# Row sums of the adjacency one graph earlier, and an earlier transpose of x1, in a two-layer graph network

## Chip, cores and metric

The kernel runs on one core of a Trainium2 chip. The metric is the device time of one execution in microseconds (us); the median of three runs is compared. The core has five engines with queues of their own: TensorE (PE, matmuls and transposes), VectorE (DVE), ScalarE (ACT), GpSimd (POOL) and SyncE (SP, which here only issues transfers).

## What is computed

64 graphs, each with 256 nodes of 256 features. Cut to what matters (`bn` is a batch norm with fixed statistics):

```python
# layer 0
deg = adj.sum(-1); deg = where(deg != 0, deg, 1.0)
d = deg ** -0.5
a_plus = d[:, :, None] * adj * d[:, None, :] + alpha * eye
x1 = layernorm(x + (a_plus @ x) @ W.T + b)
# layer 1
h = relu(bn1(conv1d(x1, 1 tap)));  h = bn2(conv1d(h, 17 taps))
x_conv = relu(h + x1)                       # along the nodes
s = x1 @ w_se.T + b_se                      # 3 columns
A = exp(-(|s_i|^2 + |s_j|^2 - 2 s_i.s_j))   # 256 x 256
x_nmp = A @ relu(x1 @ w_msg.T + b_msg)
x2 = GRU(input=concat(x_conv, x_nmp), state=x1)
out = layernorm(x1 + x2)
```

## The kernel before

**Stages.** The 64 graphs make four quarters of 16 (Q = 16). Each quarter goes through three kinds of work. First its *graphs*: layer 0 and the parts of layer 1 up to the spectrum of h. Then the *products*: the 17-tap convolution is done for all 16 graphs at once in a transformed domain, with `p_k` (L545) as its matmuls. Then the *gates*: the GRU, with `p_g` (L872) as its matmuls and a layernorm at its end. The stages of neighbouring quarters are interleaved: some graphs of the next quarter run beside products and their transforms (VectorE operations on the tile VM, L600 to L755), some beside gates of the quarter in front. In graphs 0 to 15 the place of gates is taken by the transform of the weights (`p_u`, L308). After graph 63 only the last quarter's products and gates are left.

**One graph.** `layer0(g)` is a generator in pieces that end with `yield`:

- Piece 1. The row sums (L358): two ScalarE activations that copy a half of adj to an unused place and add up each row into `deg`. The guard (L369, DVE): where the sum is 0 it becomes 1. The power `dis` (L371, POOL), deg to the power of -0.5. `adeg` (L373, DVE), alpha times deg. Four transposes `p_adjT` (L380, PE), their copy (L381, ACT), two DVE operations that put the diagonal in (L383, they need adeg), the scaling of x into `x1` (L393, ACT, twice, it needs dis), and x plus its bias (L394, POOL).
- Piece 2. `p_hT` (L401, eight matmuls, which need x1 and adjT with its diagonal), its copy (L406, ACT).
- Piece 3. `p_out0` (L411, eight matmuls, which need hT), and its two evictions into x1 (L416, DVE, which scale by dis).
- Pieces 4 and 5. The layernorm: statistics (L326 to L328, DVE), a power (L329, POOL), then L332 (DVE) and two activations (L334, ACT), and the store of x1 (L422).

`layer1(g)` has seven pieces: the transpose of x1 (`x1_transposed`, L425: four transposes `p_x1T`, L431; copies L432 and L433, ACT) | `p_conv` (L448) with the evictions L451 and L452 (ACT) and the squares of s (L456, L458, L459, DVE) | `p_msg` (L469, relu L472) | `p_dft` (L486, copies L491) | `p_rows` (L499, copies L501 and L503) | `p_dist` (L510, exp L511 on ACT, product with adjT L512 on DVE) | `p_nmp` (L519, copy L523, store L524 issued from ACT's queue).

**What sets the order.** Nothing is sorted by cost. The order of each engine's queue is that in which the generators are stepped, except where `tc.issue_after(i)` puts an instruction behind instruction i of the same engine's queue (an order, not a wait). `graphs()` (L994) steps layer1(g) and, between its pieces, steps layer0(g + 2) at places listed in PLACES (L990):

```python
PLACES = (("other",), ("layer0",), (), (), ("layer0",), ("other", "layer0"), ())
```

So row sums and transposes of adj for graph g + 2 come behind conv, p_hT behind p_rows, p_out0 behind the gates ("other") that follow the distances, the layernorm's statistics at the end of the graph (STATS) and its end in the following graph behind the relu L472 (APPLIED). PE's order in a graph is, for most graphs: p_rows, p_hT, p_dist, gates, p_out, p_nmp, p_x1T, gates, half of p_conv, p_adjT, the other half, p_msg, p_dft. In graphs 16 to 27 (the set ALONE, which stand beside no gates) p_x1T of the next graph comes between p_out and p_nmp. The row sums of graph g + 2 are put behind EVICTED[g], the last L452 of graph g, but are free to come earlier in ALONE graphs and in graphs below 16.

**Buffers.** The matmul tiles of a graph (`p_adjT`, `p_hT`, `p_out0`, `p_x1T`, `p_conv`, `p_msg`, `p_dft`, `p_rows`, `p_dist`, `p_nmp`) share four PSUM buffers in turn: a tile waits until the fourth in front of it has been read. adj_t and x_t have two buffers; their loads for graph g + 3 are issued from SP's queue at the start of graph g (L104 to L110). x1, xn, msg and the like have one or two buffers, adjT three.

Of the kernel before, what the change touches and what calls it, by code (L numbers as in the profile page):

```python
# [26 lines left out]
def kernel(  # L27
# [27 lines left out]
    nc = tc.nc  # L55
    B, N, D = x.shape
# [4 lines left out]
    DCH = D // P  # L61
# [6 lines left out]
    Q = P // GT  # L68
# [13 lines left out]
    def bank(name):  # L82
        return ps.tile([P, 512], F32, tag="bank", name=name)
# [7 lines left out]
    def mark(op, gates=0):  # L91
        marks.append((op.ins, gates))
# [226 lines left out]
    def layernorm(y, eps=LN_EPS):  # L319

        chunks = range(y.shape[1])
        st = small.tile([P, NCH, nc.vector.BN_STATS_DIM], F32, name="ln_st")
        mv = small.tile([P, NCH, nc.vector.BN_AGGR_DIM], F32, name="ln_mv")
        rs = small.tile([P, NCH], F32, name="ln_rs")
        for c in chunks:
            nc.vector.bn_stats(st[:, c, :], y[:, c, :])  # L326
            nc.vector.bn_aggr(mv[:, c, :], st[:, c, :])
        nc.vector.tensor_scalar(rs[:, : len(chunks)], mv[:, : len(chunks), 1], eps, None, op0=ALU.add)  # L328
        nc.gpsimd.tensor_tensor(rs[:, : len(chunks)], rs[:, : len(chunks)], neg_half[:, : len(chunks)], op=ALU.pow)  # L329
        yield  # L330
        mr = small.tile([P, NCH], F32, name="ln_mr")
        nc.vector.scalar_tensor_tensor(mr[:, : len(chunks)], mv[:, : len(chunks), 0], -1.0, rs[:, : len(chunks)], op0=ALU.mult, op1=ALU.mult)  # L332
        for c in chunks:
            nc.scalar.activation(  # L334
                y[:, c, :], y[:, c, :], AF.Identity, bias=mr[:, c : c + 1], scale=rs[:, c : c + 1]
            )
# [4 lines left out]
    xn_d = [dram.tile([P, 2 * DCH, N], F32, name=f"xn_d{g}") for g in range(B)]  # L341
    XN = {}
    ALONE = set()
    EVICTED, RELU = {}, {}
    ADJT, X1, X_SCALED, DIAGONAL = {}, {}, {}, {}


    def layer0(g):

        a_t, x_t = ain.pop(g), xin.pop(g)  # L350

        adjT = work.tile([P, NCH, 3, P], F32, name="adjT", bufs=3)
        ADJT[g] = adjT

        deg = small.tile([P, NCH], F32, name="deg")
        def degrees():
            for c in range(NCH):
                nc.scalar.activation(  # L358
                    unused if g >= Q else adjT[:, c, 0:2, :].rearrange("p n q -> p (n q)"), a_t[:, c, :], AF.Copy,
                    accum_out=deg[:, c : c + 1],  # L360
                )

        if g == 1 or g >= Q and g - 2 not in ALONE:

            with tc.issue_after(X_SCALED[0] if g == 1 else EVICTED[g - 2]):
                degrees()
        else:
            degrees()
        nc.vector.scalar_tensor_tensor(deg, deg, 0.0, deg, op0=ALU.is_equal, op1=ALU.add)  # L369
        dis = small.tile([P, NCH], F32, name="dis")  # L370
        nc.gpsimd.tensor_tensor(dis, deg, neg_half[:, :NCH], op=ALU.pow)  # L371
        adeg = small.tile([P, NCH], F32, name="adeg")
        nc.vector.tensor_scalar(adeg, deg, alpha_t, None, op0=ALU.mult)  # L373

        p = bank("p_adjT").rearrange("p (c n) -> p c n", c=NCH)
        for mc in range(NCH):
            for c in range(NCH):
                nc.tensor.transpose(p[:, mc, c * P : (c + 1) * P], a_t[:, c, mc * P : (mc + 1) * P], ident)  # L380
        copied = nc.scalar.copy(adjT[:, :, 0:3:2, :], p.rearrange("p c (n q) -> p c n q", q=P))  # L381
        for mc in range(NCH):
            DIAGONAL[g] = nc.vector.scalar_tensor_tensor(  # L383
                adjT[:, mc, 1, :], ident, adeg[:, mc : mc + 1], adjT[:, mc, 2 * mc, :],
                op0=ALU.mult, op1=ALU.add,
            ).ins


        x1 = work.tile([P, NCH, D], F32, name="x1")
        X1[g] = x1  # L390
        with tc.issue_after(copied.ins) if g < 2 else ExitStack():
            for c in range(NCH):
                X_SCALED[g] = nc.scalar.activation(x1[:, c, :], x_t[:, c, :], AF.Copy, scale=dis[:, c : c + 1]).ins  # L393
        nc.gpsimd.tensor_tensor(x_t, x_t, b0_t.unsqueeze(1).to_broadcast([P, NCH, D]), op=ALU.add)  # L394

        yield
        hT = work.tile([P, DCH, N], F32, name="hT", bufs=1)
        p = bank("p_hT").rearrange("p (k n) -> p k n", k=DCH)
        for k in range(DCH):
            for mc in range(NCH):  # L400
                nc.tensor.matmul(  # L401
                    p[:, k, :], x1[:, mc, k * P : (k + 1) * P],
                    adjT[:, mc, 1 - mc : 3 - mc, :].rearrange("p n q -> p (n q)"),
                    start=mc == 0, stop=mc == NCH - 1,
                )
        nc.scalar.copy(hT, p)  # L406
        yield
        p = bank("p_out0").rearrange("p (c o) -> p c o", c=NCH)
        for c in range(NCH):
            for k in range(DCH):  # L410
                nc.tensor.matmul(  # L411
                    p[:, c, :], hT[:, k, c * P : (c + 1) * P], w0[:, k, :], start=k == 0, stop=k == DCH - 1
                )
        for c in range(NCH):
            mark(
                nc.vector.scalar_tensor_tensor(  # L416
                    x1[:, c, :], p[:, c, :], dis[:, c : c + 1], x_t[:, c, :], op0=ALU.mult, op1=ALU.add
                )
            )
        yield  # L420
        yield from layernorm(x1)
        nc.scalar.dma_start(x1_d[g // Q][g % Q].rearrange("(c p) d -> p c d", p=P), x1)  # L422
        yield

    def x1_transposed(g):  # L425
        x1 = X1.pop(g)
        xn = XN[g] = work.tile([P, 2 * DCH, N], F32, name="xn")
        p = bank("p_x1T").rearrange("p (k n) -> p k n", k=DCH)
        for k in range(DCH):
            for c in range(NCH):  # L430
                nc.tensor.transpose(p[:, k, c * P : (c + 1) * P], x1[:, c, k * P : (k + 1) * P], ident)  # L431
        nc.scalar.activation(xn[:, 0], p[:, 0], AF.Identity, bias=unit, scale=others_only)  # L432
        nc.scalar.copy(xn[:, 2 * DCH - 1], p[:, 1])  # L433

    def layer1(g, place):
# [3 lines left out]
        xn, adjT = XN.pop(g), ADJT.pop(g)  # L439
# [5 lines left out]
        for c in range(NCH):  # L445
            p = bank("p_conv1")[:, : D + NSE]
# [19 lines left out]
        p = bank("p_msg").rearrange("p (c d) -> p c d", c=NCH)  # L466
# [14 lines left out]
        for k in range(DCH):  # L481
            p = bank("p_dft")

            for c, t0, t1 in ((0, 0, mid + 1), (1, mid - 1, GT)):
                first = t0 + 1 - c * mid
# [11 lines left out]
        p = bank("p_rows")  # L497
# [9 lines left out]
        for c in range(NCH):  # L507
            rows = slice(32 * c, 32 * c + 32)
            p = bank("p_dist")[:, :N]
            nc.tensor.matmul(p, dl[rows, c * P : (c + 1) * P], dr[rows, :], start=True, stop=True)  # L510
            nc.scalar.activation(aT[:, c].rearrange("p n q -> p (n q)"), p, AF.Exp, bias=nsq[:, c : c + 1], scale=2.0)  # L511
        mark(nc.vector.tensor_mul(aT, aT, adjT[:, :, 0:3:2, :]))  # L512
        yield
        if g in ALONE:
            x1_transposed(g + 1)
        p = bank("p_nmp").rearrange("p (k n) -> p k n", k=DCH)
        for k in range(DCH):
            for mc in range(NCH):
# [1 line left out]
                    p[:, k, :], msg[:, mc, k * P : (k + 1) * P], aT[:, mc].rearrange("p n q -> p (n q)"),  # L520
                    start=mc == 0, stop=mc == NCH - 1,
                )
        nc.scalar.copy(xn[:, 1 : 1 + DCH], p)  # L523
        nc.scalar.dma_start(xn_d[g], xn)  # L524
        yield

# [427 lines left out]
    def chain(*stages):  # L954
        for stage in stages:
            yield from stage
# [13 lines left out]
    def run(stage):  # L970
        for _ in stage:
            pass
# [18 lines left out]
    STATS, APPLIED = len(PLACES) - 1, 4  # L991
    ENDS = [iter(())]

    def graphs(first, part, others):  # L994


        for i in part:
            load(first + i + 3)
            given = {"layer0": layer0(first + i + 2) if first + i + 2 < B else iter(()), "other": others[i]}
            for piece, _ in enumerate(layer1(first + i, i)):  # L1000
                if piece == APPLIED:
                    with tc.issue_after(RELU[first + i]):
                        run(ENDS.pop())
                    ENDS.append(given["layer0"])
                elif piece == STATS:
                    next(given["layer0"], "end")
                yield
                for name in PLACES[piece]:
                    if next(given[name], "end") != "end":
                        yield  # L1010
            yield from given["other"]

    with tc.tile_pool(name="setup", bufs=1) as setup:
# [52 lines left out]
        others = [weights(setup, i, scale2) for i in range(NPARTS)]  # L1066
# [26 lines left out]
    def nothing():  # L1093
        return iter(())
# [16 lines left out]
    for q in range(NQ):  # L1111
        first = (q + 1) * Q
        more = q + 1 < NQ
        end = chain(complex_end(q), copies(V2) if more else iter(()))
        if more:
            if q:
                others = [take(late, 3 if i % 3 == 0 else 2) for i in range(AHEAD)]
            else:
                others = [nothing() for _ in range(AHEAD)]
# [24 lines left out]
        if more:  # L1144
# [6 lines left out]
            others = [take(early, 5 if q == 0 else 2) for _ in range(Q)]  # L1151
# [63 lines left out]
```

## Time and profile before

| what | value |
|---|---|
| median of three runs | 2073.0 us (2072.61 to 2079.12) |
| profiled execution, its own time | 2079.83 us |
| its span in the profile | 2078.0 us |
| mean TensorE clock | 0.991 of full |
| TensorE busy | 1996.5 us |
| graphs 0 to 15 | about 40 to 296 us of the span |
| graphs 16 to 27 | about 296 to 505 us |
| graphs 28 to 31 | about 505 to 610 us, then products and gates to 799 us |
| graphs 32 to 47 | about 799 to 1110 us |
| graphs 48 to 63 | about 1301 to 1611 us |
| the last products and gates | to 2078 us |

How to read it. "Busy" is the time in which an engine executes; its share is an average over stages with different limits. A line of the waits names an engine, its instruction and its source line, then, after the arrow, the engine, tile and line whose end released it, with the total in us, the number of times and the longest. "L393" is line 393 of the kernel before. A group's line gives the instructions of one line and shape, their busy time and mean duration in ns, then the idle time of the engine before them and what ended it. The chain of waits follows the work back from the end: each entry is what the next one waited for.

### The profile page before, as it was taken

How to read it: one execution, taken by the hardware profiler on the slowest of the kernel's cores; microseconds unless marked ns; L12 is line 12 of the kernel's file. 1: busy time of each engine (PE TensorE's matmuls, PEld its weight loads, DVE VectorE, ACT ScalarE, POOL GpSimd, SP SyncE). 2: the span in 40 equal slices, each digit the busy share in tenths (PEclk: the TensorE clock that was granted, in tenths of full speed). 3: DMA queues.
4: the chain of work that ended last, by engine and by line, in shares of the span. 5: the costliest groups of instructions: out<-in, count | busy, mean ns of one | idle time of the engine just before them, and what ended most of it. 6: DMA issues, size and time to landing. Idle time of an engine off the chain costs nothing.

```text
span 2078.0 us, 26334 instructions
## 1 busy us (share of the span) xinstructions
PE 1996.5 (96%) x8157; PEld 1444.4 (70%) x8157; DVE 1395.1 (67%) x3241; ACT 937.4 (45%) x2232; POOL 663.7 (32%) x672
## 2 busy tenths in 40 slices
PE   6999999998999999989999999999999999999997
PEld 5888888877677766767777766666777765555554
DVE  5444458776568897753546889774445899977776
ACT  4676644566432234555553223545554123333333
POOL 3444410122432243232322234322332124434443
PEclk9999999999999999999999999999999999999999
DMA  4765657544447644343326664433333754443331
GB/s 122 232 221 184 195 183 226 174 142 146 107 145 216 201 124 125 114 119 109 102 96 184 202 177 123 126 119 104 107 107 114 232 151 128 126 111 99 99 91 52
DMA packets 305288, 298.04 MB, mean 143 GB/s; under 512 B 84192, under 2 KB 283956, under 8 KB 305150
## 3 DMA queue, kind: packets, MB, share of 16 engines
q1 hardware_dynamic: 245198, 200.37, 33.2%
q10 hardware_dynamic: 44480, 67.39, 9.1%
q0 software_dynamic: 15472, 28.61, 6.1%
q8 instruction: 66, 1.08, 0.2%
q14 instruction: 72, 0.59, 0.1%
HBM read 193.19 MB, written 103.06 MB: 143 GB/s over the span
## 4 chain that ended last, share of the span: by engine, by line
PE 48%; DVE 12%; issue 4%; DMA 4%; POOL 3%; ACT 3%; SPq 0%; ACTq 0%; POOLq 0%; DVEq 0%
PE p_g L872 30%; PE p_k L545 7%; PE p_hT L401 3%; PE p_out L411 2%; PE p_nmp L519 2%; DMA u<-ud 2%; POOL sums L843 1%; DVE ln_st L326 1%; PE p_dist L510 1%; PE p_conv L448 1%; DVE VM L733 1%; ACT x L393 1%; POOL dis L371 1%; POOL ln_rs L329 1%; DVE G L927 1%
## 5 line engine op out<-in xcount | busy, mean ns | idle before, releaser
L872 PE MATMUL p_g<-wall,sums 128*128 128x384 f32 x1536 | 536.2, 489 | 5.6 <-DVE G L900 5.5
L872 PEld LDWEIGHTS p_g<-wall,sums 128*128 128x128 f32 x1536 | 284.4, 190 | 193.0 <-issue 12.7
L872 PE MATMUL p_g<-wall,inputs 128*128 128x384 f32 x1152 | 408.1, 490 | 7.2 <-DVE G L890 7.2
L872 PEld LDWEIGHTS p_g<-wall,inputs 128*128 128x128 f32 x1152 | 217.9, 191 | 158.0 <-DVE G L890 14.1
L843 POOL TENSOR_TENSOR sums<-inputs 128x384 f32<-128x384 f32 x128 | 142.7, 1115 | 317.7 <-PE p_g L872 265.6
L329 POOL TENSOR_TENSOR ln_rs<-ln_rs,neg_half 128x2 f32<-128x2 f32 x129 | 95.0, 738 | 400.9 <-DVE ln_rs L328 329.0
L512 DVE TENSOR_TENSOR aT<-aT,adjT 128x512 f32<-128x512 f32 x64 | 47.3, 740 | 229.1 <-ACT aT L511 229.1
L915 ACT ACTIVATE G<-G 128x512 f32<-128x512 f32 x128 | 80.7, 630 | 265.4 <-DVE G L902 154.5
L545 PE MATMUL p_k<-u,VM 128*128 128x256 f32 x736 | 175.3, 381 | 5.0 <-DMA u<-ud 4.9
L545 PEld LDWEIGHTS p_k<-u,VM 128*128 128x128 f32 x736 | 138.7, 190 | 32.4 <-DMA u<-ud 4.2
L401 PE MATMUL p_hT<-adjT,x 128*128 128x256 f32 x512 | 130.8, 400 | 18.0 <-ACT x L393 7.7
L394 POOL TENSOR_TENSOR x_t<-x_t,b_t 128x512 f32<-128x512 f32 x64 | 89.5, 1399 | 158.5 <-issue 92.1
L448 PE MATMUL p_conv<-wc,xn 128*128 128x259 f32 x512 | 125.3, 383 | 6.4 <-ACT xn L432 5.7
L371 POOL TENSOR_TENSOR dis<-deg,neg_half 128x2 f32<-128x2 f32 x64 | 47.5, 743 | 254.1 <-DVE deg L369 251.3
L411 PE MATMUL p_out<-w,hT 128*128 128x256 f32 x512 | 124.6, 387 | 4.1 <-ACT hT L406 3.7
L401 PEld LDWEIGHTS p_hT<-adjT,x 128*128 128x128 f32 x512 | 95.2, 197 | 40.2 <-ACT x L393 10.7
L519 PE MATMUL p_nmp<-aT,msg 128*128 128x256 f32 x512 | 121.6, 380 | 0.2 <-DVE aT L512 0.2
L469 PE MATMUL p_msg<-wmsg,xn 128*128 128x256 f32 x512 | 121.2, 379 | 0.0
L411 PEld LDWEIGHTS p_out<-w,hT 128*128 128x128 f32 x512 | 97.1, 193 | 32.2 <-ACT hT L406 12.8
L486 PE MATMUL p_dft<-fwd,h 128*128 128x240 f32 x512 | 114.4, 366 | 1.9 <-ACT scols L452 1.9
L448 PEld LDWEIGHTS p_conv<-wc,xn 128*128 128x128 f32 x512 | 95.6, 190 | 29.0 <-ACT xn L432 7.5
L843 POOL TENSOR_TENSOR sums<-inputs,sums 128x384 f32<-128x384 f32 x64 | 68.9, 1077 | 133.9 <-PE p_g L872 133.8
(163 smaller groups left out, 3535.7 us busy)
## 6 DMA issues: line engine op xcount, KB each, us to landing
u<-ud SPq DMA_DIRECT2D x284, 256.0 KB
xn_d<-xn ACTq DMA_DIRECT2D x64, 512.0 KB
inputs<-xn_d SPq DMA_DIRECT2D x64, 512.0 KB
ud<-u_set POOLq DMA_DIRECT2D x39, 480.0 KB, 6.2
adj_t<-in_adj_dram SPq DMA_DIRECT2D x64, 256.0 KB
x_t<-in_x_dram SPq DMA_DIRECT2D x64, 256.0 KB
x_d<-x ACTq DMA_DIRECT2D x64, 256.0 KB
xc_d<-VM SPq DMA_DIRECT2D x64, 256.0 KB
```

Of the source, the lines that this page charges most:

```text
L329: nc.gpsimd.tensor_tensor(rs[:, : len(chunks)], rs[:, : len(chunks)], neg_half[:, : len(chunks)], op=ALU.pow)
L394: nc.gpsimd.tensor_tensor(x_t, x_t, b0_t.unsqueeze(1).to_broadcast([P, NCH, D]), op=ALU.add)
L401: nc.tensor.matmul(p[:, k, :], x1[:, mc, k * P : (k + 1) * P], adjT[:, mc, 1 - mc : 3 - mc, :].rearrange("p n q -> p (n q)"), start=mc == ...
L411: nc.tensor.matmul(p[:, c, :], hT[:, k, c * P : (c + 1) * P], w0[:, k, :], start=k == 0, stop=k == DCH - 1)
L448: nc.tensor.matmul(p, x1T[:, k, c * P : (c + 1) * P], wc1[:, k, :], start=k == 0, stop=k == DCH - 1)
L469: nc.tensor.matmul(p[:, c, :], x1T[:, k, c * P : (c + 1) * P], wmsg[:, k, :], start=k == 0, stop=k == DCH - 1)
L486: nc.tensor.matmul(p[:, t0 * FL : t1 * FL], h[:, c, k * P : (k + 1) * P], fwd[:, first : first + t1 - t0, :].rearrange("p t f -> p (t f)") ...
L519: nc.tensor.matmul(p[:, k, :], msg[:, mc, k * P : (k + 1) * P], aT[:, mc].rearrange("p n q -> p (n q)"), start=mc == 0, stop=mc == NCH - 1,)
L545: nc.tensor.matmul(p[:, j * D : (j + 1) * D], v[:, k, :], u[:, k, :], start=k == 0, stop=k == DCH - 1)
L843: nc.gpsimd.tensor_tensor(S[i], x, y, op=op)
L872: nc.tensor.matmul(p[:, : 3 * HD] if k == 0 else p[:, HD:], a[:, k], wall[:, b, k].rearrange("p t d -> p (t d)"), start=first and k == 0, ...
L915: nc.scalar.activation(rz, rz, AF.Tanh, scale=0.5)
```

## The change

Three things change their places; no instruction is added or taken out.

1. The row sums, guard, power and adeg become a piece of layer0 of their own for every graph after the first two. They are issued for graph g + 3 at the end of graph g, after the layernorm statistics of graph g + 2, with the row sums behind AGGREGATED[g], the nmp copy of graph g in ACT's queue. Graph 2's are issued ahead of graph 0. What is left of the first piece (p_adjT, its copy, the diagonal, the scaling of x) stays at its place, two graphs ahead and behind conv, as before.
2. The scaling of x (L393) of graph g is put behind EVICTED[g - 2] in ACT's queue, the last copy of the conv evictions.
3. p_x1T of graph g + 1 with its copies comes behind the distances of graph g, ahead of p_out0, in the graphs of a list (EAGER): 0, 12 to 14, 16 to 28, 37, 38, 53 and 54. In the others it stays at the start of the next graph. ALONE is filled but no longer read.

```diff
-    EVICTED, RELU = {}, {}
+    EAGER = {0, Q - 4, Q - 3, Q - 2, *range(Q, Q + 13), 2 * Q + 5, 2 * Q + 6, 3 * Q + 5, 3 * Q + 6}
+    EVICTED, RELU, AGGREGATED, LAYER0 = {}, {}, {}, {}
...
-        if g == 1 or g >= Q and g - 2 not in ALONE:
-
-            with tc.issue_after(X_SCALED[0] if g == 1 else EVICTED[g - 2]):
-                degrees()
-        else:
+        at = X_SCALED[0] if g == 1 else AGGREGATED.get(g - 3)
+        with tc.issue_after(at) if at else ExitStack():
             degrees()
         nc.vector.scalar_tensor_tensor(deg, deg, 0.0, deg, op0=ALU.is_equal, op1=ALU.add)
         dis = small.tile([P, NCH], F32, name="dis")
         nc.gpsimd.tensor_tensor(dis, deg, neg_half[:, :NCH], op=ALU.pow)
         adeg = small.tile([P, NCH], F32, name="adeg")
         nc.vector.tensor_scalar(adeg, deg, alpha_t, None, op0=ALU.mult)
+        if g > 1:
+            yield
...
-        with tc.issue_after(copied.ins) if g < 2 else ExitStack():
+        with tc.issue_after(copied.ins if g < 2 else EVICTED[g - 2]):
             for c in range(NCH):
                 X_SCALED[g] = nc.scalar.activation(x1[:, c, :], x_t[:, c, :], AF.Copy, scale=dis[:, c : c + 1]).ins
...
         mark(nc.vector.tensor_mul(aT, aT, adjT[:, :, 0:3:2, :]))
-        yield
-        if g in ALONE:
+        if g in EAGER:
             x1_transposed(g + 1)
+        yield
...
-        nc.scalar.copy(xn[:, 1 : 1 + DCH], p)
+        AGGREGATED[g] = nc.scalar.copy(xn[:, 1 : 1 + DCH], p).ins
...
+    def of_layer0(g):
+        if g not in LAYER0:
+            LAYER0[g] = layer0(g) if g < B else iter(())
+        return LAYER0[g]
+
     def graphs(first, part, others):
         for i in part:
             load(first + i + 3)
-            given = {"layer0": layer0(first + i + 2) if first + i + 2 < B else iter(()), "other": others[i]}
+            if first + i == 0:
+                next(of_layer0(2))
+            given = {"layer0": of_layer0(first + i + 2), "other": others[i]}
...
                 elif piece == STATS:
                     next(given["layer0"], "end")
+                    next(of_layer0(first + i + 3), "end")
```

## Prediction on record

> **What bounds the kernel now.** I read the page's busy shares first, then TensorE's waits, then the groups behind the largest waits, then the chain of waits around the worst place.
>
> ```profile
> span 2078.0 us, 26334 instructions
> PE 1996.5 (96%) x8157; PEld 1444.4 (70%) x8157; DVE 1395.1 (67%) x3241; ACT 937.4 (45%) x2232; POOL 663.7 (32%) x672
> ```
>
> TensorE (PE) is busy for 1996.5 of 2078.0 us, so the change, which takes no matmul away, can only work on the 81.5 us in which PE stands, and on stretches in which PE runs slowly. The waits of PE name what ended each idle stretch (sum, times, longest):
>
> ```profile
> PE p_hT L401 <- ACT x L393: 7.7, 9, 1.8
> PE p_g L872 <- DVE G L890: 7.2, 7, 1.6
> ...
> PE p_conv L448 <- ACT xn L432: 5.7, 7, 1.1
> ...
> PE p_hT L401 <- ACT msg L472: 4.7, 18, 0.8
> PE p_rows L499 <- DVE deg L369: 3.9, 2, 2.0
> PE p_hT L401 <- DVE adjT L383: 3.8, 6, 1.3
> PE p_out L411 <- ACT hT L406: 3.7, 6, 0.9
> ```
>
> The first, fourth and fifth belong to the row-sum chain, the third and last to x1's transpose. The gate waits (L890) are mostly in the last stage, where no graph runs; the change does not reach them. The groups behind the first (busy, mean ns | idle of that engine before it, and its releasers):
>
> ```profile
> L393 ACT ACTIVATE x<-x_t,dis 128x256 f32<-128x256 f32 x128 | 60.1, 507 | 47.3 <-POOL dis L371 47.3
> L371 POOL TENSOR_TENSOR dis<-deg,neg_half 128x2 f32<-128x2 f32 x64 | 47.5, 743 | 254.1 <-DVE deg L369 251.3
> ```
>
> ACT stands 47.3 us ahead of the scaling L393 waiting for the power, and POOL stands ahead of the power for the guard L369: the power comes just in time or too late. The chain of waits at the worst place (start, us, what):
>
> ```profile
> 917.64 0.58 ACT xn L432
> 918.27 1.14 PE p_conv L448 x4
> ...
> 922.46 1.37 POOL ln_rs L329 x2
> 923.83 0.97 POOL sums L843
> 924.87 0.99 POOL sums L843
> 926.02 0.72 POOL dis L371
> 926.76 0.52 ACT x L393
> 927.33 3.78 PE p_hT L401 x8
> 931.11 1.16 PE p_dist L510 x4
> ```
>
> In graph 38 PE waits 1.08 us for L432, 1.96 us before p_rows and 0.79 us before p_hT; then the eight p_hT matmuls take 3.78 us, where the same eight take 1.73 us at 961.44. The same picture stands at 1420 to 1429 (graph 54). And as a table of stages (sum; PE, PEld, DVE, ACT, POOL busy; clock):
>
> ```profile
> 296.00:505.00 209.00, 201.73 (x985) 169.00 (x984) 155.94 (x409) 113.18 (x292) 34.30 (x32) 1.00 0.53 171
> 799.00:961.00 162.00, 154.01 (x653) 113.54 (x652) 100.67 (x275) 86.94 (x225) 44.19 (x48) 0.97 0.38 114
> ```
>
> PE stands 7.3 us in graphs 16 to 27 and 8.0 us in graphs 32 to 39. DVE at 156 of 209 us is dense in the first of these stretches.
>
> **What the Trainium skill says.** "Perfetto Trace Analysis", section "Tensor Engine Instruction (MATMUL, LD_WEIGHTS)": ScalarE, VectorE and GpSimd are strict FIFO. The trace agrees: at 923.93 ACT has nothing to do but L393, and L491, whose p_dft was ready by 924.1, starts at 927.58, after it. "TensorE: Matmul & The Clock Gate", "Part 1: The HAM clock gate": after an idle window of about 3.4 us the clock goes to half, and to full again after a busy window; the windows run freely. The trace agrees with that: PE is nearly idle from 924.07 to 927.33 (3.26 us), then runs at half rate from 927.33 to 936.20.
>
> **The change, part by part.** Nothing is added to or taken from any engine's work; the instruction orders of both kernels have equal counts.
>
> *Row sums, guard, power and adeg, one graph earlier.* Each graph's two row sums (430 ns each, with an accumulator read of 0.19 us) now stand behind the nmp copy L523 of the graph three in front. Every instruction counts on its queue:
> - ACT: 2 × (0.43 + 0.19) = 1.24 us between L523 and what followed it, L432/L433 or L451. In a gate graph, 897.39: L523 0.58, L432 0.57, L433 0.37 end at 898.76 and would end at 900.0; conv starts at 901.50. Cover 1.5 us, from 3.9 us of gate matmuls. In graphs 2 to 11 four p_u program matmuls and x1T cover about 3.4 us against a chain of 2.8 us. Price 0; if the cover went, up to 1.2 us a graph.
> - DVE: L369 and L373 (0.15 + 0.25 us) move from beside L383 to behind layernorm's L332, ahead of L456. They could stall the queue until ACT has summed, but ACT is done by nmp's end + 1.9 us, and L332 waits for POOL L329 longer than that anyway (449.01, with nmp's end at 444.75). Price 0 to 0.4 us in graphs 16 to 27.
> - POOL: the power (0.74 us) leaves the place behind sums L843 and comes behind L329.
> - The row sums now need adj(g+3) earlier. Its load is issued 16 us (graph 0), then 24 us or more, before the end of L523 of graph g; the three times ACT waited for it, it came 2.9 to 4.2 us after issue. No wait.
>
> L393 then waits only for its place behind L452. Where its stall goes:
> - p_hT<-x apart from graphs 38 and 54, 7.7 − 2 × 0.79 = 6.1 us: at 887.21 (and 1388) the wait of 1.81 becomes one of 0.9 for L383, next in line on DVE. Gain 6.1 − 1.8 = 4.3.
> - p_hT<-msg, 4.7: L472 stands behind L393 in ACT's queue, as at 979 and 1097. Next late is p_rows, which PE does first. I take 4.0.
> - p_hT<-adjT of graphs 34 and 50, 0.59 and 0.58, and half of p_rows<-ln_mv (0.41 + 0.42): 1.6. The other adjT waits stay.
>
> *x1T between distances and out0.* The four transposes (0.44 us) move ahead of out0 in 21 graphs (in 12 of them, 16 to 27, from between out0 and nmp, in the others from behind nmp).
> - conv<-L432: five waits of 0.70 (49, 240, 253, 268, 515 us) go, since p_out and p_nmp (3.5 us) now stand between transpose and conv: 3.5.
> - out<-hT waits at 263, 401 and 510 (0.78, 0.90, 0.76) are filled by 0.44 of transposes each: 1.3.
> - In graph 0 it also lets part of the 1.7 us wait for taps pass: 0 to 1.7, I take 0.8.
>
> *Graphs 38 and 54, both parts together.* Before: 1.08 + 1.96 + 0.79 = 3.83 us. The conv wait goes, but p_rows then stands ready earlier, and its columns still wait for L458/L459 on DVE, behind L332, behind POOL's L329 and L843. POOL's second inputs move forward there, so I let the columns come 0.7 us earlier (bounds 0 and 1.5) and the 0.79 vanish: 1.5 each, 3.0. The half-rate stretch costs (936.20 − 927.33)/2 ≈ 4.4 us each time; PE would still stand about 2.3 us there around a short p_rows, so I keep it.
>
> *Graphs 16 to 27.* In 16 to 19 products of the transform cover all. In 20 to 27 waits of 1.18, 0.77 and 0.21 for the distances may lose 1.0; the loop out0 → L416 → layernorm → L456 → L383 → p_hT takes 0.44 us more for x1T ahead of out0, against some 0.3 us of L369/L373 out of its middle. Bounds −4 and +4 over the stretch; I take 0.
>
> *New waits.* In graph 27, at 503, row sums join the copies between the two spectrum buffers ahead of L451, and p_dft<-scols (1.92) may grow: +0.5. In graph 37 p_adjT and p_msg wait for banks freed later: +0.35 each place and quarter, +0.7.
>
> Sum: 4.3 + 4.0 + 1.6 + 3.5 + 1.3 + 0.8 + 3.0 − 0.5 − 0.7 = 17.3 us. Made against the profiled execution's own time, 2079.8 (span 2078.0 + 1.8 outside), this is 2062.5; the median of the runs is 2073.0, 6.8 below, and the same waits are in those runs: 2073.0 − 17.3 = 2055.7.
>
> **Rivals.**
> - *The half clock vanishes too* (2046). If PE's idle time near 924 falls apart into less than a window, both half-rate stretches go: 2 × 4.4 = 8.8, so 2055.7 − 8.8 = 2047, with luck in graphs 20 to 27 2046. For it: the idle shrinks from 3.26 us. Against it: the window runs freely and p_rows is only 0.2 us of work; what remains may still fill one.
> - *The waits are moved, not removed* (2067). p_hT then waits for L383, msg or POOL instead of L393, and p_rows for all that conv saved. Only the five conv waits and the fillings of 1.3 and 0.8 remain: 5.6, thus 2067. For it: at 926 the p_rows wait is named for DVE deg though L459 ended 0.1 us before; against it: 47.3 us of ACT's idle time is named for the power alone.
> - *Slower* (2084): ACT's 1.24 us behind L523 reaches conv. One mechanism: L432 and L433 stand behind the row sums in 28 gate graphs, and gate activations behind DVE (0.63 us each) join them. It decides where they take more than the 1.5 us of cover; two do, with 1.26 + 1.24 = 2.5 us, so 1.0 us a graph, 28 us, less 17.3: +10.7. For it: at 917.64 L432 was late behind just such an activation (L931). Against it: in the built order most graphs have no gate activation between L523 and L433.
> - *It does not do what it says*: excluded by the built order, in which the row sums stand behind L523 in every later graph and p_x1T ahead of p_out in the listed ones.
>
> **How the numbers follow.** Forecast (2056; own range 2050 to 2063) 0.50; half clock gone 0.17; waits moved 0.20; slower 0.10; anything else 0.03. The range 2043 to 2074 reaches over the clock and the moved case with the bounds of graphs 20 to 27, and leaves out mainly the slower one. Of this kernel a measurement can tell about 0.3%, 6.2 us: below 2066.8 is faster. All of the first two, half of the third and a rest give 0.78; the other half of the third gives 0.11; slower 0.11.
>
> **What would show it.** Right: L393's 47 us for L371 gone; p_conv<-xn down to the setup's; p_hT<-msg near 1; one p_rows wait of 2 to 3 us in graphs 38 and 54; TensorE's busy time unchanged if the half clock stays and some 9 us less if not. Wrong: p_conv<-xn with many short waits (the row sums reach conv), or p_hT<-adjT grown in graphs 20 to 31.

## The result: 2086.6 us, slower, and the profile after

| | before | after |
|---|---|---|
| median (five runs each, one chip) | 2075.47 us (2072.61 to 2079.15) | 2086.64 us (2086.41 to 2091.76) |
| ratio of the runs | | 1.0058, 95% interval 1.0039 to 1.0078 |
| profiled execution: own time, span | 2079.83, 2078.0 us | 2086.43, 2084.5 us |

The change costs about 12 us where 17 us less were forecast. Of that the two profiled executions show 6.5 us, since the one of before is at the slow end of its runs and the one of after at the fast end of its own. The shares on top of the page of the changed kernel:

```profile
span 2084.5 us, 26346 instructions
...
PE 1994.9 (96%) x8157; PEld 1446.3 (69%) x8157; DVE 1420.8 (68%) x3241; ACT 932.9 (45%) x2232; POOL 662.7 (32%) x672
```

(The 12 instructions more than before are waits in the engines' queues; the counts of the engines' own work are the same.) PE is busy for 1.6 us less and stands for 8 us more. DVE executes the same 3241 instructions in 25.7 us more: they have become longer, which a mere change of order should not do. 12.9 of these are the subtraction L313 of the weight transform, 10.6 the diagonal operations L383. TensorE's waits after:

```profile
PE p_rows L499 <- DVE scols L459: 11.6, 5, 4.2
PE p_hT L401 <- DVE adjT L383: 10.4, 11, 1.8
PE p_out L411 <- ACT hT L406: 9.7, 9, 5.6
...
PE p_dft L486 <- ACT scols L452: 3.3, 1, 3.3
PE p_nmp L519 <- DVE aT L512: 3.2, 5, 0.8
...
PE p_hT L401 <- ACT msg L472: 0.4, 1, 0.4
...
PE p_hT L401 <- ACT x L393: 0.2, 1, 0.2
```

What the change was to take away is away: 7.7 us behind the scaling are 0.2, 4.7 behind the relu are 0.4, and the waits of conv for L432 (5.7) have left the list. In their place stand the diagonal (10.4 for 3.8), hT's copy (9.7 for 3.7), the columns of p_rows (11.6), and p_nmp for aT (3.2 for 0.2). TensorE's clock also differs: it was half from 402.9 to 406.3, 515.5 to 518.9, 577.0 to 583.8, 1655.6 to 1659.0 and 1775.1 to 1778.5 us, and full in the same places before. An estimate of the cost, half of PE's busy time in each, is 1.7, 1.5, 2.4, 1.7 and 1.7 us.

Where it came from, by the start of each graph's p_rows in the two traces (after less before, us):

| stretch | difference | forecast |
|---|---|---|
| to graph 4 | +0.3 | −1.5 |
| graphs 4 to 11 | +7.9 | 0 |
| graphs 12 to 15 | −4.7 | about −3 |
| graphs 16 to 27 | +10.4 | 0 (−4 to +4) |
| graphs 28, 29 | −3.3 | about −2 |
| graphs 30, 31 with products and gates | +7.0 | 0 |
| graphs 32 to 47, and 48 to 63 | −9.5, −4.8 | −5 each |
| last products and gates | +3.2 | 0 |

The last stretch has no graphs in it. The two half-clock stretches there are as much as its +3.2, and it differs by up to 8 us between the runs below (480.1 us in experiment 3, 488.1 in experiment 2); nothing more is made of it. The losses sit in three places.

**Graphs 20 to 27: the diagonal.** The timeline of DVE, then of POOL, in graph 23 of the changed kernel (start, us, then what ran and the idle time before it):

```profile
444.57 0.42 DVE L635 SCALAR_TENSOR_TENSOR turn<-VM 128x256 f32<-128x256 f32 x1
444.91 1.62 DVE L383 SCALAR_TENSOR_TENSOR adjT<-ident,adeg,adjT 128x128 f32<-128x128 f32 x2
446.44 0.68 DVE L705 SCALAR_TENSOR_TENSOR VM<-turn,VM 128x512 f32<-128x512 f32 x1
```

```profile
442.98 0.72 POOL L369 TENSOR_TENSOR dis<-deg,neg_half 128x2 f32<-128x2 f32 x1 [0.34 <-DVE deg L367]
444.77 1.34 POOL L394 TENSOR_TENSOR x_t<-x_t,b_t 128x512 f32<-128x512 f32 x1 [1.07 <-issue]
```

The same in graph 24 of the kernel before, POOL, then DVE:

```profile
434.17 0.71 POOL L371 TENSOR_TENSOR dis<-deg,neg_half 128x2 f32<-128x2 f32 x1
...
444.82 1.51 POOL L394 TENSOR_TENSOR x_t<-x_t,b_t 128x512 f32<-128x512 f32 x1 [9.28 <-issue]
```

```profile
445.20 0.39 DVE L326 BATCH_NORM_STATS2 ln_st<-x 128x6 f32<-128x256 f32 x1
445.51 1.36 DVE L713 SCALAR_TENSOR_TENSOR turn<-turn 128x512 f32<-128x512 f32 x1
...
451.31 0.60 DVE L383 SCALAR_TENSOR_TENSOR adjT<-ident,adeg,adjT 128x128 f32<-128x128 f32 x2
```

Two diagonal operations take 1.62 us in the changed kernel, 0.60 before. The first of them can't get on while POOL adds the bias to x, from 444.77 to 446.11, and p_hT, which needs it, starts at 446.41. Over the whole kernel the group of the diagonal operations grew from 366 to 445 ns in the mean; 12 of its 128 are longer by 1.0 us, all beside L394 (before it was one, at 52.8). Five of the 12 lie in graphs 22 to 27, the other seven in graphs 31 and later. PE's waits for the diagonal in graphs 20 to 27 add up to 9.1 us where they were 1.3. The Trainium skill has the rule, in "SBUF — State Buffer", "Who interferes with whom": a DVE instruction with two SBUF inputs contends with a GpSimd instruction that reads SBUF, since they share ports, which are an exclusive lock. L383 has two SBUF inputs, ident and adjT, and L394 reads x_t and the bias. The trace agrees: the stretched L383 ends at 446.26, 0.15 us after L394. And it isn't every DVE operation that suffers. Before, beside the same L394, L713 with two SBUF inputs took 1.36 us, twice its median of 0.68, while L326, with one, took its usual 0.39.

What moved L394 into this place is not an earlier power but a later one. Before, the row sums of these graphs were bound to nothing and ran ahead: the power ended 15.3 us ahead of graph 24's p_rows (450.20), and L394 ended 3.9 us ahead of it, clear of the diagonal. In the changed kernel the row sums stand behind AGGREGATED; the power ends at 443.70, 0.8 us ahead of graph 23's p_rows, L393 starts at 443.73 and ends by 444.64, and L394 starts 0.13 us later, just ahead of the diagonal. ACT's waits for the power say the same:

```profile
ACT x L393 <- POOL dis L369: 25.3, 16, 3.4
```

Before they were 47.3 us, none of them in graphs 16 to 27; now eight, with 10.8 us, are in graphs 16 to 26. "One graph earlier" holds in time only from graph 28 on (in graph 41 the power ends 4.5 us ahead of p_rows instead of 0.9). In graphs 4 to 12 it ends about 4.4 us ahead instead of 9.4. The seven stretched operations in graphs 31 and later are beside a scaling that did come earlier.

**Graphs 4 to 11: a transfer overtakes another.** POOL in the weight transform, in graph 3 of the kernel before and of the changed one:

```profile
95.44 0.71 POOL L371 TENSOR_TENSOR dis<-deg,neg_half 128x2 f32<-128x2 f32 x1 [6.04 <-DVE deg L369]
96.13 2.98 POOL L314 TENSOR_TENSOR u_set<-u_set,u_set 120x1024 f32<-120x1024 f32 x1
99.41 1.11 POOL L316 DMA_DIRECT2D ud<-u_set  x2 [0.30 <-POOL u_set L314]
```

```profile
94.33 2.38 POOL L314 TENSOR_TENSOR u_set<-u_set,u_set 120x1024 f32<-120x1024 f32 x1 [4.64 <-ACT u_set L311]
97.00 0.55 POOL L316 DMA_DIRECT2D ud<-u_set  x1 [0.30 <-POOL u_set L314]
```

Before, the power held POOL until DVE had begun its subtraction L313 (95.67), and the add L314 ended at 99.11. Now the power comes behind the add (100.79) and nothing is in front of it; it starts first and ends at 96.71. DVE's subtraction beside it takes 3.37 us (94.41) instead of 1.22. POOL's stores of the weights (480 KB each) are on their way from 97.0, ahead of the next taps loads; before, three of these were issued (98.18 to 99.59) by the time the first store went (99.4). SP's queue before, then of the changed kernel:

```profile
98.18 1.41 SPq L291 DMA_DIRECT2D taps<-in_conv2T_dram  x3
```

```profile
98.64 0.38 SPq L110 DMA_DIRECT2D x_t<-in_x_dram  x1
99.07 6.69 SPq L291 DMA_DIRECT2D taps<-in_conv2T_dram  x3
```

The three issues that took 1.4 us before take 6.7. The taps come late, their scaling L300 waits 6.74 us for them at the head of DVE's queue (till 110.94), and aT's product L512 and p_nmp behind it are late; hT's copy comes late behind the store L422 in ACT's queue. Of the 7.9 us, 5.8 are waits of PE at p_out and p_nmp in graphs 4, 6, 8 and 10. That the stores are what slows the issues is read from this order of events; no run moves the stores alone.

**Graph 30: hT's copy behind the gates' inputs.** ACT and POOL of the changed kernel:

```profile
577.92 0.51 ACT L821 ACTIVATE inputs<-inputs,bn_bias 128x256 f32<-128x256 f32 x1 [7.78 <-POOL inputs L818]
578.45 0.58 ACT L406 COPY hT<-p_hT 128x512 f32<-128x512 f32 x1
```

```profile
575.36 1.23 POOL L808 DMA_DIRECT2D xc_g<-x_d  x1 [7.24 <-DMA inputs<-x_d]
576.18 1.70 POOL L818 TENSOR_TENSOR inputs<-inputs 128x512 f32<-128x512 f32 x1
```

p_hT had ended at 570.7. Its copy stands behind L821, as it did before (L821 at 562.18, the copy at 562.71). L821 needs POOL's L818, which stands behind the accumulating transfer L808 in POOL's queue, and L808 starts when the loads of the gate's inputs have landed. New is that these loads come late against the graph, whose p_rows starts at 557.96 before and at 568.61 after. SP's queue before, then of the changed kernel:

```profile
554.16 0.36 SPq L799 DMA_DIRECT2D x_g<-x_d  x1
554.58 0.46 SPq L788 DMA_DIRECT2D xc_g<-xc_d  x1
556.37 0.52 SPq L795 DMA_DIRECT2D inputs<-x_d  x1
```

```profile
568.16 0.36 SPq L799 DMA_DIRECT2D x_g<-x_d  x1
568.58 0.46 SPq L108 DMA_DIRECT2D adj_t<-in_adj_dram  x1
569.14 2.34 SPq L788 DMA_DIRECT2D xc_g<-xc_d  x1
571.59 0.52 SPq L795 DMA_DIRECT2D inputs<-x_d  x1
```

L795, whose landing releases L808, was issued 1.6 us ahead of p_rows and is now issued 3.0 us behind it. Of these 4.6 us, 3.4 are there at L799 already, which waits for the landing of the store L850 of an earlier output (until 554.03 before, 568.01 after). 0.6 is the adj load of graph 34, which the rebuilt order puts ahead of L788, and 0.7 lies between L788, now issued over 2.34 us, and L795.

### The profile page after: what moved, and what is told of

Read it like the earlier page. It is cut to its first block, busy times and chain, and to the rows that moved or that the text cites. A ratio compares the mean times of both kernels' runs of the same rounds, so it can differ in the third digit from the quotient of the medians.

```text
span 2084.5 us, 26346 instructions
## 1 busy us (share of the span) xinstructions
PE 1994.9 (96%) x8157; PEld 1446.3 (69%) x8157; DVE 1420.8 (68%) x3241; ACT 932.9 (45%) x2232; POOL 662.7 (32%) x672
## 3 DMA queue, kind: packets, MB, share of 16 engines
q8 instruction: 66, 1.08, 0.2%
## 4 chain that ended last, share of the span: by engine, by line
PE 61%; DVE 12%; DMA 4%; issue 1%; ACT 1%; POOL 1%; SPq 0%; POOLq 0%; ACTq 0%; DVEq 0%
PE p_g L872 33%; PE p_k L545 7%; PE p_hT L401 4%; PE p_out L411 3%; PE p_nmp L519 3%; PE p_conv L448 2%; PE p_msg L469 2%; PE p_dft L486 2%; PE p_dist L510 1%; DMA u<-ud 1%; DVE VM L733 1%; PE p_x1T L431 1%; DMA inputs<-xn_d 1%; DVE ln_st L326 1%; DVE turn L627 1%
## 5 line engine op out<-in xcount | busy, mean ns | idle before, releaser
L329 POOL TENSOR_TENSOR ln_rs<-ln_rs,neg_half 128x2 f32<-128x2 f32 x129 | 97.3, 755 | 529.0 <-DVE ln_rs L328 441.8
L843 POOL TENSOR_TENSOR sums<-inputs 128x384 f32<-128x384 f32 x128 | 141.1, 1102 | 338.7 <-PE p_g L872 258.9
L512 DVE TENSOR_TENSOR aT<-aT,adjT 128x512 f32<-128x512 f32 x64 | 46.5, 727 | 215.9 <-ACT aT L511 215.9
L401 PE MATMUL p_hT<-adjT,x 128*128 128x256 f32 x512 | 130.8, 399 | 14.1 <-DVE adjT L383 10.4
L394 POOL TENSOR_TENSOR x_t<-x_t,b_t 128x512 f32<-128x512 f32 x64 | 85.3, 1333 | 123.0 <-ACT x L393 90.1
L843 POOL TENSOR_TENSOR sums<-inputs,sums 128x384 f32<-128x384 f32 x64 | 68.8, 1075 | 143.2 <-PE p_g L872 142.9
L892 ACT COPY G<-p_g 128x512 f32<-128x512 f32 x64 | 37.4, 584 | 167.5 <-PE p_g L872 135.5
```

The lines of the kernel that those rows point to most:

```text
L401: nc.tensor.matmul(p[:, k, :], x1[:, mc, k * P : (k + 1) * P], adjT[:, mc, 1 - mc : 3 - mc, :].rearrange("p n q -> p (n q)"), start=mc == ...
L843: nc.gpsimd.tensor_tensor(S[i], x, y, op=op)
```

## The experiments

The line numbers of the variants can be shifted by a few lines.

**1. The bias addition behind the diagonal.** The element that POOL first reads costs POOL 0.18 us a graph in the median; the engines' other queues keep their order.

```diff
+        seen = small.tile([P, 1], F32, name="seen")
+        look = nc.gpsimd.tensor_copy(seen, adjT[:, NCH - 1, 1, 0:1])
+        with tc.issue_after(look.ins):
-        nc.gpsimd.tensor_tensor(x_t, x_t, b0_t..., op=ALU.add)
+            nc.gpsimd.tensor_tensor(x_t, x_t, b0_t..., op=ALU.add)
```

> The changed kernel, but POOL's addition of the bias to x (x_t plus b0) must first read one element of what the second diagonal operation of the graph wrote, so that it can't run beside the diagonal operations on DVE. Theory A (the earlier power lets the scaling of x end early, POOL's addition then starts just ahead of the diagonal operation, which has two SBUF inputs as it has, and holds it off for 1.0 us on the path to p_hT in graphs 20 to 31): the 12 stretched diagonal operations of 1.35 us fall to 0.35 us and the time falls by 6 to 9 us from the changed kernel's, to about 2079. Rival B (the loop is longer because x1's transpose stands ahead of out0): within 2 us of the changed kernel.

Measured 2069.4 us, ratio to before 0.9963 (0.9948 to 0.9978): 17 below the changed kernel (20 by the ratios to before, since the runs are from different chips), at least twice what was expected. Graphs 20 to 27 are 8 us faster. The "earlier power" of the expectation is wrong for these graphs, as is the "late power" that experiments 8 and 10 speak of there; the collision is what it says. The same place in its trace, DVE:

```profile
447.06 0.61 DVE L383 SCALAR_TENSOR_TENSOR adjT<-ident,adeg,adjT 128x128 f32<-128x128 f32 x2
447.58 0.69 DVE L708 SCALAR_TENSOR_TENSOR VM<-turn,VM 128x512 f32<-128x512 f32 x1
448.31 1.78 DVE L709 SCALAR_TENSOR_TENSOR VM<-turn,VM 128x512 f32<-128x512 f32 x1
```

The diagonal is back at 0.61 us. The lock has not gone: the operation L709 on VM now pays (1.78 where its neighbour takes 0.69), but p_hT doesn't wait for it. The rest came in places where I had not counted the collision: p_rows of graphs 34 and 50 (1.08 us to 0.12), p_hT in 36 and 52 (1.25 to 0.35 or less), and p_rows of 38 and 54 (4.16 to 3.07). Graphs 4 to 11, which this order doesn't touch, took 6.3 us more in this profiled execution than in the changed kernel's, at the same waits; its other runs are faster, down to 2065.7.

**2. Row sums alone.** x1's transpose at its old places.

```diff
-        if g in EAGER:
-            x1_transposed(g + 1)
         yield
+        if g in ALONE:
+            x1_transposed(g + 1)
```

> The changed kernel with the row sums early, but x1's transpose where it was before (between out0 and nmp in graphs 16 to 27, else behind the graph). Theory A: graphs 20 to 27 stay as slow as in the changed kernel and the conv waits of 0.7 us come back: about 2090. Rival B (the transpose's place is what costs in graphs 20 to 27): these graphs are as fast as before, about 2080.

2111.6 us, ratio 1.0168 (1.0145 to 1.0190). Worse than expected by 21, but on the side of theory A: graphs 20 to 27 wait for the diagonal as in the changed kernel, so the transpose's place isn't what costs there. Four conv waits for L432, behind graphs 12, 13, 14 and 28, take 1.6 us each, where they took 0.7 before: the two row sums between L523 and L432 are worth 0.9 us wherever only p_x1T covers them. The moved transpose is what pays for the moved row sums. Most of the rest is in graphs 0 to 3, 12 us more than in the changed kernel (with waits of 3.9 us at p_u and 3.2 at p_nmp), and in gates that wait 4.4 us for their inputs in each of graphs 37 and 53; why is open.

**3. The transpose alone.** The kernel before with the list EAGER in place of ALONE for p_x1T.

> The kernel before with only the transpose of x1 moved, to the changed kernel's list; row sums and power stay where they were. Theory A: the five conv waits of 0.7 us and part of the out0 waits go, nothing is lost in graphs 4 to 10 or 20 to 27: about 2070, 5 below the kernel before. Rival B: graphs 20 to 27 lose their 7 us here: about 2080.

2064.7 us, ratio 0.9949 (0.9930 to 0.9969): faster, and more than forecast for it. In the trace graphs 4 to 11 are without a wait, graphs 12 to 15 4.9 us faster, and graphs 38 and 54 run at full clock: 4.8 us each, so a good part of the gain is the clock's. In graph 30 p_out waits 1.9 us for hT, with the adj load behind the gate's loads: part of the loss there comes with the transpose.

**4. Old row sums up to graph 13.**

```diff
+        if 1 < g < Q - 2:
+            yield
-        at = X_SCALED[0] if g == 1 else AGGREGATED.get(g - 3)
+        at = X_SCALED[0] if g == 1 else AGGREGATED.get(g - 3) if g >= Q - 2 else None
...
-        if g > 1:
+        if g >= Q - 2:
             yield
```

> The changed kernel, with the row sums, guard and power of graphs 2 to 13 at the old place and without the order for the scaling of x there. Theory A2 (the 8 us lost in graphs 4 to 10 come from the row sums' move, through the order in which transfers reach the queues): about 2079. Rival B2 (they come from the transpose's move in graph 0, which puts the order of p_u and the taps off): within 2 us of the changed kernel, 2086.

2077.5 us, ratio 0.9997 (0.9986 to 1.0007): 9 below the changed kernel. PE has no wait in graphs 4 to 11. The loss there comes from the row sums' move; the transpose of graph 1 stands where the change put it.

**5. POOL's add behind DVE's subtraction.** This tests the chain itself: only 13 small reads on POOL are added, every other queue keeps the order of the changed kernel.

```diff
+                seen = pool.tile([1, 1], F32, name="seen_u", bufs=2)
+                look = nc.gpsimd.tensor_copy(seen, us[3][0:1, 0, 0:1])
+                with tc.issue_after(look.ins):
-                nc.gpsimd.tensor_tensor(us[2], us[0], us[1], op=ALU.add)
+                    nc.gpsimd.tensor_tensor(us[2], us[0], us[1], op=ALU.add)
```

> The changed kernel, but in the weight transform POOL's add of two u sets must first read one element of what DVE's subtraction of the same sets wrote. Theory A3 (without the power in front of it, POOL's add starts ahead of the subtraction in every second graph, ends 2.4 us earlier and sends its three stores of 480 KB ahead of the next taps loads, whose issue then takes 3 us each; taps scaling, aT and p_nmp come late, and so does the x1 store in front of hT's copy): the waits of graphs 4 to 10 go, 8 us less than the changed kernel, about 2079. Rival B3 (one more gate-weight load ahead of the taps loads in SP's queue is the cause): within 2 us of the changed kernel's 2087, since that order stays.

2079.9 us, ratio 1.0013 (0.9996 to 1.0030): 7 below the changed kernel. Its POOL in graph 3:

```profile
96.77 0.17 POOL L315 COPY seen_u<-u_set 1x1 f32<-1x1 f32 x1 [6.02 <-DVE u_set L313]
96.91 2.35 POOL L317 TENSOR_TENSOR u_set<-u_set,u_set 120x1024 f32<-120x1024 f32 x1
99.21 1.06 POOL L319 DMA_DIRECT2D ud<-u_set  x2
```

Counted from the graph's p_rows (91.23 here, 90.16 in the changed kernel) the first store goes 1.1 us later, and the scaling of the taps waits at most 1.2 us instead of 6.7. PE has no wait in graphs 4 to 11. The cause is the order of add and stores, not the gate-weight load in SP's queue, which stayed. The edit takes away the long subtraction and the early stores together; which of the two counts is read from the waits alone.

**6. Both orders on POOL.**

> The changed kernel with both orders on POOL: bias addition behind the diagonal, and add behind subtraction in the weight transform. If the two losses are separate places, the gains add: 17 and 8 below the changed kernel's 2087, about 2062. Rival (the first already contains the second, or a new wait takes their place): 2069 or more.

2059.1 us, ratio 0.9915 (0.9886 to 0.9945). The gains add, and with both collisions gone the change makes the kernel 0.85% faster, some 18 us. That this is close to the forecast's 17 is luck in part: it contains what the order of the bias addition gains by itself (experiment 8), and the loss of graph 30. The longest of TensorE's waits for hT is that one:

```profile
PE p_out L417 <- ACT hT L412: 6.2, 5, 4.8
```

**7. Row sums early from graph 34 on, with the moved transpose and the bias behind the diagonal.**

```diff
+        early = g >= 2 * Q + 2
+        if g > 1 and not early:
+            yield
...
```

> The transpose's list of the changed kernel, the row sums early only for graphs 34 and later (that is, at the end of graph 31 and later), the bias addition behind the diagonal. Theory A (early sums help only in the gate graphs, by 1.5 us in graphs 32 to 38 and 4 us in 39 to 48, twice): 5 to 11 us below the transpose alone (2065), about 2057. Rival (the gain seen there was the clock's, not the sums'): 2065.

2054.5 us, ratio 0.9895 (0.9869 to 0.9922). Against the transpose alone, graphs 32 to 63 gain some 13 us in the traces, part of it the clock's; graphs 20 to 26, whose row sums are at their old places, gain 3 from the order of the bias addition (experiment 10 takes it away). Graphs 28 to 31 lose 6 in turn. Early row sums are worth their place where gates cover them.

**8. The control: the kernel before with the bias behind the diagonal.**

> The kernel before with only the bias addition behind the diagonal operations. Theory A (before, the late power kept the bias addition off the diagonal operations, so that there was nothing to mend): within 2 us of the kernel before, 2078. Rival (the order is a gain of its own, whatever the row sums do): 5 to 10 us less, about 2070.

2072.8 us, ratio 0.9973 (0.9957 to 0.9989): 0.27%, some 5.6 us less. That is outside theory A's 2 us and at the near end of the rival's 5 to 10. Its profiled span (2077.5) is that of before to 0.5 us, but the traces differ: the waits of p_hT for the diagonal in graphs 34 and 50 (0.6 us each) are gone, and the half-clock stretches at graphs 38 and 54 last 6.8 and 3.4 us instead of 10.2. A start 2 us later, a last stage 2 us longer and other half-clock stretches hide that in the span. So the order has a gain of its own, of which the trace explains a part; the larger part of the 17 us of experiment 1 is the collision that the change made.

**9. hT's copy ahead of the inputs' bias.** The kernel of experiment 6, with one load from another queue:

```diff
-        nc.sync.dma_start(ain[g], adj[g].rearrange("(c p) m -> p c m", p=P))
+        (nc.scalar if g == 34 else nc.sync).dma_start(ain[g], adj[g].rearrange("(c p) m -> p c m", p=P))
```

> The kernel with both POOL orders (2059), with one edit in graphs 30 and 31: the load of adj for graph 34 is issued from ACT's queue instead of SP's. With it the planner also puts the copy of hT (graph 30) ahead of the gate inputs' bias in ACT's queue, so two things change there. Theory A (hT's copy stands 5 us behind the bias activation L821, which waits for inputs that come late): the wait of p_out in graph 30 goes, 4 to 5 us less, about 2055. Rival (the gate matmuls behind wait for the same inputs instead): 2059.

2055.5 us, ratio 0.9896 (0.9879 to 0.9912). The wait of 4.85 us in graph 30 is gone, 0.5 comes back at a gate, and the trace is 6.6 us ahead from graph 32 on. Of the two edits the trace gives the load the smaller share: the inputs' bias starts 6.9 us behind p_rows instead of 8.6, while hT's copy, no longer behind it, starts at 2.2. The intervals of experiments 6 and 9 overlap, so the gain is shown by the trace of graph 30 and not by the medians.

By the end the two traces are equal again (spans of 2052.0 and 2052.1 us): 4.5 us are lost in graph 54 and 2.8 in the last stage. PE in graph 54 in the kernel of experiment 6, then of 9:

```profile
1412.58 0.41 PE L505 MATMUL p_rows<-ident,scols 128*128 128x128 f32 x2 [3.07 <-DVE scols L465]
1412.83 1.89 PE L407 MATMUL p_hT<-adjT,x 128*128 128x256 f32 x8
```

```profile
1405.46 0.66 PE L505 MATMUL p_rows<-ident,scols 128*128 128x128 f32 x2 [3.08 <-DVE scols L465]
1405.91 3.62 PE L407 MATMUL p_hT<-adjT,x 128*128 128x256 f32 x8
```

The same order on PE, the same wait of 3.1 us, and once the clock falls to half (0.51 from 1405 to 1415) and once it doesn't (1.00 from 1412 to 1422).

**10. As 7, but with the bias addition free.**

> Row sums early from graph 34 and the moved transpose, but the bias addition free as in the changed kernel. Theory A (in graphs 20 to 31 the late power still keeps the addition off the diagonal; in the gate graphs the early one meets it, but the gates cover some of that): 0 to 5 us more than with the order (2054.5), about 2058. Rival (the collision costs as much in gate graphs as in graphs 20 to 31, 1 us in each of 28): 2075 or more.

2061.4 us, ratio 0.9929 (0.9912 to 0.9945): 7 above experiment 7, 2 more than theory A allows and far from the rival. Seven diagonal operations are stretched by 1 us, all in graphs 33 and later. In graphs 20 to 27 none is, though the bias addition is free: with the row sums back at their old, earlier places these graphs take 107.6 us, 117.9 in the changed kernel.

**11. As 7, with the load of experiment 9.** The lowest median here.

> Row sums early from graph 34, bias addition behind the diagonal (2054.5), and the adj load of graph 34 from ACT's queue, with which hT's copy comes ahead of the inputs' bias in graph 30. Theory A: the wait of 2.5 us for hT's copy in graph 30 goes: about 2052. Rival: 2054.5, since later gates wait for the inputs.

2051.1 us, ratio 0.9872 (0.9854 to 0.9891), 1.3% below the kernel before. In graph 30 the wait of 2.5 us became one of 1.0 for aT. The inputs' bias comes no sooner than in experiment 7 (7.8 us behind p_rows, 6.9 there), so here it is the place of hT's copy that counts. The interval overlaps that of experiment 7.

## Why the prediction was wrong, step by step

- *What it removes.* Right in mechanism, and nearly in size. PE's waits behind L393, L472 and L432 went. Graphs 12 to 15, 28, 29 and 32 to 63 gained 22 us in the traces; the sum had 17.3 in all. 9.5 of the 22 are in graphs 37, 38, 53 and 54, where the clock has a share.
- *"Row sums, guard, power and adeg, one graph earlier."* This step failed for graphs 2 to 12 and 16 to 27. The prediction read from the sum of 47.3 us that the power comes just in time or too late, and took that for all graphs. In these graphs ACT had no such wait; their row sums ran ahead, and the new order holds them back (at the place shown, the power ends 0.8 us ahead of p_rows instead of 15.3).
- *"POOL: the power leaves the place behind sums L843 and comes behind L329."* This step failed too. In graphs 2 to 11 there are no sums L843; what the power leaves is the place ahead of the add L314. The step follows the power to its new place and doesn't ask what POOL does sooner once the power is out of its way. L314 starts ahead of DVE's subtraction: +7.9 us where the step on graphs 2 to 11 says "Price 0". That step counted ACT's cover of 3.4 us, which held; the loss came through POOL's stores and the taps.
- *Graphs 16 to 27: "Bounds −4 and +4 over the stretch; I take 0."* +10.4. The loop was counted by instruction durations from the trace of before. A duration was taken to belong to an instruction, and it belongs to an instruction and to what runs beside it. L394, which L393 releases, is in no step, though the text itself gains the time at which L393 starts; so its meeting with the diagonal is missing, which took PE's waits there from 1.3 to 9.1 us. The half clock at 402.9 and 515.5 adds some 3 us (estimate above). The 0.44 us of x1T in the loop were no cause (experiments 2 and 3).
- *"The row sums now need adj(g+3) earlier ... No wait."* Right for the row sums. But the loads are in an order rebuilt with the rest, and in graph 30 those of the gate's inputs come 4.6 us later against the graph, with hT's copy behind them: +7.0 with graph 31.
- *Graphs 38 and 54.* Forecast −1.5 each with the half clock kept; the pairs 37, 38 and 53, 54 gave −6.4 and −3.1. p_rows waits 4.2 us, more than the 2 to 3 named; the half-clock stretch of 10.2 us fell to 3.4 in graph 38 and stayed in graph 54. The rival of the vanishing half clock was partly true and was outweighed.
- *"Slower: ACT's 1.24 us behind L523 reaches conv."* Right sign, wrong mechanism: no wait of conv for L432 is left. Experiment 2 shows that it would have been true without the moved transpose.
- *New waits.* p_dft behind L452 in graph 27: forecast +0.5, measured +1.4.

Shown by taking it away: both POOL orders (experiments 1, 5 and 6), the row sums' move as their origin (4 and 10), and graph 30's wait (9). Read from traces alone: that the early stores slow the taps' issues, and what makes the gate's loads late in graph 30. Open: part of the 5.6 us of experiment 8, and the rest of experiment 2.

## What to carry to other kernels

Before an operation is moved, look in the trace, stage by stage, at where it runs now: a place that is earlier in the program can be later in time. Then, whichever way it moves, list what its readers release in turn, on every engine, and ask what those will run beside. Two-input DVE operations on the critical path and large GpSimd operations should be kept apart by an order, not by the accident of their times; one element read of the result that has to come first is enough. And an engine that becomes free sooner also sends its transfers sooner, ahead of others that were needed first.

## What the hardware showed beside that

A read of one element on POOL cost 0.17 us for one partition (experiment 5), and 0.18 us in the median for 128 partitions (experiment 1; 0.45 in the mean, the longest of 64 being 6.3 us); either was well repaid. TensorE's clock after the same idle time of 3.1 us fell to half in one execution and not in another, 4.5 us of difference in 16.7; "TensorE: Matmul & The Clock Gate", "Part 1: The HAM clock gate" calls its window free-running, and these two traces agree. The half-clock stretches in the traces of before, after and experiments 6 and 9, the one at the end of each apart, last 3.4, 6.8 or 10.2 us. Single runs of one kernel differ by more than such a stretch costs (2053.9 to 2065.4 us in experiment 6); how much of that is the clock isn't shown.
